# Loading the next group's x in halves behind stores, and another order of the last normalisations

## The chip, the cores and the metric

The kernel runs on one core of a Trainium2 chip. The metric is the device time of one execution in microseconds (us); six runs of the kernel before have a median of 277.8 us, from 277.44 to 279.92. The engines are named as the profile names them: PE (matrix multiply; PEld is its weight load), DVE (vector), ACT (scalar activations), POOL, and SP, whose queue issues nearly all transfers.

## What is computed

One cross-attention layer. x is (16, 256, 256), the context is (16, 77, 192), with 8 heads of 256 columns. All is float32.

```python
Q = (img_embed @ Wq).reshape(B, -1, H, D).transpose(0, 2, 1, 3)
K = (sent_embed @ Wk).reshape(B, -1, H, D).transpose(0, 2, 1, 3)
V = (sent_embed @ Wv).reshape(B, -1, H, D).transpose(0, 2, 1, 3)
score = jnp.einsum('bhqd,bhkd->bhqk', Q, K) / math.sqrt(D)
mask = (atten_mask != 0)[:, None, None, :]
score = jnp.where(mask, score, -jnp.inf)
attn = jax.nn.softmax(score, axis=-1)
ctx = jnp.einsum('bhqk,bhkd->bqhd', attn, V).reshape(B, -1, H * D)
out = ctx @ Wo + img_embed
mu = jnp.mean(out, axis=-1, keepdims=True)
var = jnp.var(out, axis=-1, keepdims=True)
return (out - mu) * jax.lax.rsqrt(var + EPS) * gamma + beta
```

## The kernel before

**Tiles and groups.** The 16 x 256 rows of x are 32 tiles of 128 rows, `t` = 0 to 31, two for each batch. Four batches (eight tiles) make a group `g` = 0 to 3. Each group of x is loaded twice: `load_x` (L140) brings the natural rows into `xg`, in one transfer of 1 MB; there the products are added and the result is normalised and stored. `load_xT` (L160) brings the same rows in an order from which a block transpose on DVE (`transpose_x`, L170) makes the transposed x for the scores; it is four transfers of 256 KB, 1 MB in all.

**Folded weights.** A start-up of some 54 us folds Wq with Wk (`gA`, `gB`) and Wv with Wo (`uA`, `uB`). After that each batch needs `a` (context times the first fold, `prepare_a`, a quarter of the next group's per step), `vw` (context times the second, `prepare_vw`), the scores, the softmax and the product with `vw`.

**The loop** (L857) has 16 steps, `b` = -1 to 14. Step `b` does the scores (L307) of the `new` tiles, those of batch b+1; DVE adds the mask's bias and takes the row maxima (`shift`, L323); ACT does the exponentials (L339); DVE sums and POOL scales (`weigh`, L346); DVE transposes the result (`turn`, L364). Meanwhile PE works at `vw` and `a` for later and then at the products of the `now` tiles, those of batch b: `seven` (L416) for batches 0 to 10, plain `attend` (L374) for the last five. The `old` tiles, those of batch b-1, get their statistics (`finish`, L479), their reciprocal deviation by two small ACT operations (`spread`, L492) and their normalisation (`normalise`, L522). Every engine works through its instructions in the order in which this code names them; that order is written by hand.

**Two ways to normalise.** The plain way is two DVE operations (L518 in `centre`, and L534). The way called `aside` takes the small factor `less` (L508, on POOL, or on DVE where `less_on` says so), one ACT operation (L528) and two POOL operations (L529, L530). When both tiles of a batch are done, a store of 256 KB is issued on SP (L541); the two last tiles are stored one by one (L946).

**The SP queue** works in order too: a store that waits for its normalisation holds up whatever is named behind it. A step counter `n = (b+1) % 4` places the preparation of the next group `g = (b+1)//4 + 1`. Both loads of that group are named in the step with n = 0 (L871), that is in steps -1, 3 and 7; the transposes of that x come in the steps with n = 2 (tiles 0 to 3 of the group) and n = 3 (tiles 4 to 7), late on DVE (L898). The scores of the group begin one step later. The natural rows are first read two steps after n = 3, by `add_product` (L475).

**The end.** In the last step (b = 14) `old` is tiles 26 and 27, `now` is 28 and 29, `new` is 30 and 31. The statistics of 26 and 27 stand between the exponentials of 30 and 31, and their normalisation behind `turn(30)` (L919). After the loop come the two last products and the last four normalisations: 28 and 31 on DVE, 29 and 30 aside.

Of the kernel before, what the change touches and what calls it, by code (L numbers as in the profile page):

```python
# [15 lines left out]
P = 128  # L16
# [37 lines left out]
def kernel(  # L54
# [13 lines left out]
    nc = tc.nc  # L68
    B, S, DI = x.shape
# [3 lines left out]
    NG = B // GB  # L73
    QT = S // P
    NT = B * QT
    GT = GB * QT
    NF = H // 2
    KR = S2 - KM
    BK = 32
    NM = P // BK  # L80
# [47 lines left out]
    xg_of = {}  # L128

    x_rows = x.rearrange("b (t p) d -> p (b t) d", p=P)  # L130
    out_rows = out.rearrange("b (t p) d -> p (b t) d", p=P)
    c_rows = c.rearrange("b k l -> (b k) l").rearrange("(r p) l -> p r l", p=CR)

    def flat(ap):
        return ap.rearrange("p a b -> p (a b)")
# [4 lines left out]
    def load_x(g):  # L140
        xg_of[g] = const.tile([P, GT, DI], F32, tag=f"xg{g}", name=f"xg_{g}")
        nc.sync.dma_start(xg_of[g], x_rows[:, g * GT : (g + 1) * GT, :])
# [12 lines left out]
    xT_of, a_of, vw_of, p_of, mv_of = {}, {}, {}, {}, {}  # L155

    def in_two(name, shape, g):
        return pools[g % 2].tile(shape, F32, tag=f"{name}{g % 2}", name=f"{name}_{g}", bufs=1)

    def load_xT(g):  # L160

        xT_of[g] = in_two("xT", [P, GT * NM, 2, BK], g)
        rows = x.rearrange("b s d -> (b s) d")[g * GT * P : (g + 1) * GT * P, :]
        rows = rows.rearrange("(m r) (i n) -> i r m n", r=BK, i=NM)
        for i in range(NM):
            nc.sync.dma_start(
                xT_of[g][i * BK : (i + 1) * BK].rearrange("p m n q -> p m (n q)"), rows[i]
            )

    def transpose_x(g, j):  # L170
# [136 lines left out]
    def scores(t):  # L307
        g = t // GT
        j, bl = t % GT, (t // QT) % GB
        ps = [ps_mm.tile([P, 512], F32, tag="mm", name=f"ps_{t}_{a}") for a in range(2)]  # L310
        for m in range(NM):
            for dc in range(2):
                for i in range(NM):
                    nc.tensor.matmul(  # L314
                        ps[m // 2][i * BK : (i + 1) * BK, m % 2 * 2 * S2 : (m % 2 + 1) * 2 * S2],
                        xT_of[g][:, j * NM + m, dc],
                        flat(a_of[g][:, dc, bl, 2 * i : 2 * i + 2, :]),
                        start=(dc == 0),
                        stop=(dc == 1),
                    )  # L320
        ps_of[t] = ps
# [153 lines left out]
    def add_product(t):  # L475
        y = xg_of[t // GT][:, t % GT, :]
        nc.vector.tensor_tensor(y, po_of.pop(t), y, ALU.add)  # L477

    def finish(t):  # L479
        if t in po_of:  # L480
            add_product(t)
        g, j = t // GT, t % GT
        y = xg_of[g][:, j, :]
        bn = st.tile([P, 6], F32, tag="bn", name=f"bn_{t}")
        nc.vector.bn_stats(bn, y)
        if j == 0:
            mv_of[g] = st.tile([P, GT, 2], F32, tag="mv", name=f"mv_{g}", bufs=2)
        nc.vector.bn_aggr(mv_of[g][:, j, :], bn)
# [3 lines left out]
    def spread(first, last):  # L492

        g, lo, hi = first // GT, first % GT, (last - 1) % GT + 1
        log = st.tile([P, GT], F32, tag="log", name=f"log_{first}")
        rstd = st.tile([P, GT], F32, tag="rstd", name=f"rstd_{first}")
        nc.scalar.activation(log[:, lo:hi], mv_of[g][:, lo:hi, 1], AF.Ln, bias=eps)
        nc.scalar.activation(rstd[:, lo:hi], log[:, lo:hi], AF.Exp, scale=-0.5)
        all_rstd_of[first, last] = rstd

    def invert(first, last, aside=(), less_on=nc.gpsimd):

        g = first // GT
        rstd = all_rstd_of.pop((first, last))
        if aside:
            less = st.tile([P, GT], F32, tag="less", name=f"less_{first}")
            for j in (t % GT for t in aside):
                less_on.tensor_scalar(  # L508
                    less[:, j : j + 1], mv_of[g][:, j, 0:1], rstd[:, j : j + 1], -1.0,
                    ALU.mult, ALU.mult,  # L510
                )
        for t in range(first, last):
            j = slice(t % GT, t % GT + 1)
            rstd_of[t] = rstd[:, j], less[:, j] if aside else None

    def centre(t):
        y = xg_of[t // GT][:, t % GT, :]
        nc.vector.scalar_tensor_tensor(  # L518
            y, y, mv_of[t // GT][:, t % GT, 0:1], gam, ALU.subtract, ALU.mult
        )  # L520

    def normalise(t, aside=False, centred=False):  # L522

        g, j = t // GT, t % GT
        rstd, less = rstd_of.pop(t)
        y = xg_of[g][:, j, :]
        if aside:
            nc.scalar.activation(y, y, AF.Identity, bias=less, scale=rstd)  # L528
            nc.gpsimd.tensor_tensor(y, y, gam, ALU.mult)  # L529
            nc.gpsimd.tensor_tensor(y, y, bet, ALU.add)  # L530
        else:
            if not centred:
                centre(t)
            nc.vector.scalar_tensor_tensor(y, y, rstd, bet, ALU.mult, ALU.add)  # L534
        if t >= NT - QT:
            return
        done.append(t)
        if t ^ 1 in done:
            t |= 1
            j |= 1  # L540
            nc.sync.dma_start(  # L541
                out_rows[:, t + 1 - QT : t + 1, :], xg_of[g][:, j + 1 - QT : j + 1, :]
            )
# [312 lines left out]
    last = NT - 1  # L856
    for b in range(-1, B - 1):  # L857
        old = range(max(b - 1, 0) * QT, b * QT)
        now = range(max(b, 0) * QT, (b + 1) * QT)
        new = range((b + 1) * QT, (b + 2) * QT)  # L860
        for t in new:
            scores(t)
        for t in new:
            shift(t)
        for n in range(0, 2) if b < 0 else range(b + 2, min(b + 3, B // 2)):
            turn_last(n)
        g, n = (b + 1) // GB + 1, (b + 1) % GB
        work = [prepare_vw(b + 1)]
        if g < NG:
            work.append(prepare_a(g, (n,)))  # L870
            if n == 0:  # L871
                load_xT(g)
                load_x(g)
        for part_A, _, _ in work:
            part_A()
        for _, part_B, _ in work:
            part_B()
        for i, t in enumerate(new):
            exponential(t)
            if old:  # L880
                finish(old[i])
            weigh(t)
        if old:
            spread(old[0], old[-1] + 1)
        for _, _, copies in work:
            for dst, src in copies():
                nc.scalar.copy(dst, src)  # L887
        if b + 1 < NS:
            differences(b + 1)
        if b < NS:  # L890
            if now:
                seven(b)
            if old:
                invert(old[0], old[-1] + 1)
                normalise(old[0])
            for t in new:
                turn(t)
            if n >= NF - 2:  # L898
                for j in range((n - NF + 2) * GT // 2, (n - NF + 3) * GT // 2, 2):
                    transpose_x(g, j)  # L900
            if old:
                normalise(old[1])
            if now:
                add_seven(b)
            if b + 1 < NS:
                sums(b + 1)
            continue
        for t in now:
            attend(t)
        if b < B - 2:  # L910
            invert(old[0], old[-1] + 1, aside=old[:1])
            normalise(old[0], aside=True)
            turn(new[0])
            normalise(old[1])
            turn(new[1])
            for t in now:
                add_product(t)
        else:
            turn(new[0])  # L919
            invert(old[0], old[-1] + 1, aside=old)  # L920
            for t in old:
                normalise(t, aside=True)
            turn(new[1])
            for t in now:
                finish(t)
            spread(now[0], now[-1] + 1)

    for t in new:  # L930
        attend(t)
    centre(last - 3)
    invert(last - 3, last - 1, aside=(last - 2,), less_on=nc.vector)
    normalise(last - 2, aside=True)
    finish(last - 1)
    spread(last - 1, last)
    normalise(last - 3, centred=True)
    invert(last - 1, last, aside=(last - 1,), less_on=nc.vector)
    normalise(last - 1, aside=True)
    finish(last)  # L940
    spread(last, NT)
    centre(last)
    invert(last, NT)
    normalise(last, centred=True)
    for t, queue in ((last - 1, nc.scalar), (last, nc.sync)):
        queue.dma_start(out_rows[:, t, :], xg_of[NG - 1][:, t % GT, :])  # L946


# [29 lines left out]
```

## Time and profile before

| what | value |
|---|---|
| median of six runs | 277.8 us |
| the profiled execution's own time | 279.26 us |
| its span in the trace | 277.4 us |
| lies around the span | 1.86 us |
| mean granted PE clock | 0.997 of full |
| bytes read / written | 17.57 MB / 4.19 MB |

Busy time of the engines in the span: PE 268.1 us (97%), DVE 210.5 (76%), POOL 160.9 (58%), ACT 131.4 (47%).

How to read it: a page of the profile shows one execution. A list of the chain of waits goes back from the last instruction, at each step to what released it; "issue" in it is time in which an engine waited for nothing that the profile shows. A view by windows gives, for chosen stretches, the busy time of each engine with the number of its instructions, the granted PE clock, the mean busy share of the 16 DMA engines (packets that overlap can take it above 1) and the rate in GB/s. A packet is counted whole in one window.

### The profile page before, as it was taken

To read this page: it belongs to the slowest core of one execution; us is meant where nothing else is said; L and a number is where in the kernel's file an instruction comes from. 1 tells how busy PE (TensorE), PEld (TensorE's weight loads), DVE (VectorE), ACT (ScalarE), POOL (GpSimd) and SP (SyncE) were. 2 spreads that over 40 slices of the span, in tenths; PEclk is the share of its full clock that TensorE was granted. 3 is DMA by queue.
4 is the path that set the end of the run, shared out by engine and by line. 5 is a ranking of instruction groups with operands and counts; after the bars stand their busy time and mean duration, and the time that the engine had idled before them with its cause. 6 is when DMAs were issued, how large, how long until landed. Compare 5 with 4: busy or idle time off the path is not lost.

```text
span 277.4 us, 13331 instructions
## 1 busy us (share of the span) xinstructions
PE 268.1 (97%) x5972; PEld 191.3 (69%) x5972; DVE 210.5 (76%) x406; ACT 131.4 (47%) x417; POOL 160.9 (58%) x221
## 2 busy tenths in 40 slices
PE   7999999999999999989999999899999999999992
PEld 7856487867595959486959595787777767584650
DVE  0363966697649898969798888678787978879885
ACT  2303212355728281817373736455554644827552
POOL 1000007919677878785878777677787537244284
PEclk9999999999999999999999999999999999999998
DMA  6987999992000102940101019400101010110103
GB/s 182 249 191 186 329 167 161 234 166 86 2 6 2 43 2 67 174 149 4 43 2 43 2 51 191 145 2 6 41 4 43 2 43 2 40 40 2 41 2 117
DMA packets 40202, 22.63 MB, mean 82 GB/s; under 512 B 23168, under 2 KB 38608, under 8 KB 40144
## 3 DMA queue, kind: packets, MB, share of 16 engines
q1 hardware_dynamic: 40000, 21.64, 36.1%
q8 instruction: 47, 0.77, 1.2%
q10 hardware_dynamic: 144, 0.13, 0.1%
q14 instruction: 11, 0.09, 0.1%
HBM read 17.57 MB, written 4.19 MB: 78 GB/s over the span
## 4 chain that ended last, share of the span: by engine, by line
PE 90%; DVE 3%; DMA 2%; ACT 2%; issue 1%; POOL 1%; SPq 0%; DVEq 0%; POOLq 0%
PE ps L314 24%; PE pa L197 12%; PE pv L239 9%; PE po L430 9%; PE pm L430 7%; PE pa L211 6%; PE pv L250 6%; PE po L379 5%; PE pu L704 3%; PE pr L273 2%; DMA wq_nat<-in_L_xattn_Wq_dram 2%; ACT e L343 2%; PE pg L747 1%; PE pgb L704 1%; PE pw L718 1%
## 5 line engine op out<-in xcount | busy, mean ns | idle before, releaser
L343 ACT ACTIVATE e<-s,top 128x77 f32<-128x77 f32 x256 | 67.2, 347 | 74.1 <-DVE top L336 74.1
L357 POOL TENSOR_TENSOR p<-e,rden 128x512 f32<-128x512 f32 x64 | 47.3, 759 | 48.7 <-DVE rden L351 39.9
L314 PE MATMUL ps<-a,xT 128*32 128x154 f32 x2048 | 70.5, 294 | 0.8 <-issue 0.8
L314 PEld LDWEIGHTS ps<-a,xT 128*32 128x32 f32 x2048 | 66.2, 110 | 2.9 <-issue 2.0
L329 DVE TENSOR_TENSOR s<-ps,bias 128x308 f32<-128x308 f32 x64 | 30.3, 476 | 19.4 <-PE ps L314 19.4
L197 PE MATMUL pa<-cA,gA 128*32 128x308 f32 x512 | 36.1, 423 | 0.0
L463 POOL TENSOR_TENSOR xg<-xg,m 128x256 f32<-128x256 f32 x33 | 24.2, 732 | 12.6 <-DVE xg L477 10.9
L197 PEld LDWEIGHTS pa<-cA,gA 128*32 128x32 f32 x512 | 17.7, 110 | 19.6 <-issue 7.1
L239 PE MATMUL pv<-uA,cA 128*32 128x512 f32 x256 | 30.7, 592 | 0.0
L367 DVE STREAM_TRANSPOSE pT<-p 128x640 f32<-128x640 f32 x32 | 25.5, 817 | 2.4 <-POOL p L357 2.3
L349 DVE TENSOR_REDUCE den<-e 128x8 f32<-128x616 f32 x32 | 24.7, 772 | 3.4 <-ACT e L343 3.4
L336 DVE TENSOR_REDUCE top<-s 128x8 f32<-128x616 f32 x32 | 25.4, 795 | 1.1
L887 ACT COPY vw<-pv 128x512 f32<-128x512 f32 x32 | 17.1, 586 | 8.7 <-PE pv L250 8.7
L534 DVE SCALAR_TENSOR_TENSOR xg<-xg,rstd,bet 128x256 f32<-128x256 f32 x25 | 19.5, 782 | 2.2 <-ACT vw L887 0.5
L393 POOL TENSOR_TENSOR ts<-vw 128x768 f32<-128x768 f32 x11 | 20.2, 1839 | 0.0
L211 PE MATMUL pa<-cB,gB 64*32 64x308 f32 x512 | 19.5, 420 | 0.0
L379 PE MATMUL po<-vw,pT 128*32 128x256 f32 x320 | 19.2, 380 | 0.0
L477 DVE TENSOR_TENSOR xg<-po,xg 128x256 f32<-128x256 f32 x32 | 12.1, 413 | 7.6 <-PE po L430 7.2
L211 PEld LDWEIGHTS pa<-cB,gB 64*32 64x32 f32 x512 | 9.7, 107 | 11.3 <-issue 7.6
L250 PE MATMUL pv<-uB,cB 64*32 64x512 f32 x256 | 17.4, 601 | 0.0
L430 PE MATMUL po<-vr,pT 128*32 128x128 f32 x352 | 16.2, 273 | 1.2 <-issue 1.2
L887 ACT COPY a<-pa 128x308 f32<-128x308 f32 x48 | 16.8, 455 | 0.0
(112 smaller groups left out, 382.3 us busy)
## 6 DMA issues: line engine op xcount, KB each, us to landing
xT<-in_x_dram SPq DMA_DIRECT2D x16, 256.0 KB, 8.1
xg<-in_x_dram SPq DMA_DIRECT2D x4, 1024.0 KB, 9.5
out_dram<-xg SPq DMA_DIRECT2D x15, 256.0 KB, 2.3
wo<-in_L_xattn_Wo_dram SPq DMA_DIRECT2D x4, 512.0 KB, 5.2
wvT<-in_L_xattn_Wv_dram SPq DMA_DIRECT2D x16, 96.0 KB, 3.2
wq_nat<-in_L_xattn_Wq_dram SPq DMA_DIRECT2D x2, 512.0 KB, 6.3
wq_blk<-in_L_xattn_Wq_dram SPq DMA_DIRECT2D x8, 128.0 KB, 4.7
wk_blk<-in_L_xattn_Wk_dram SPq DMA_DIRECT2D x8, 96.0 KB, 5.8
```

The lines of the kernel that those rows point to most:

```text
L197: nc.tensor.matmul(flat(o[i * BK : (i + 1) * BK]), gA[:, h, cols(dc, i)], flat(cA[:, batches, :]), start=not B_first, stop=B_first,)
L211: nc.tensor.matmul(flat(banks[j + k][i * BK : (i + 1) * BK]), gB[half(k), h % NF, cols(dc, i)], flat(cB[half(k), batches, :]), start=B_fir ...
L239: nc.tensor.matmul(pv[k][i * BK : (i + 1) * BK], cA[:, b, k * BK : (k + 1) * BK], uA[:, parts, :, i], start=True, stop=False,)
L250: nc.tensor.matmul(pv[k][i * BK : (i + 1) * BK], cB[half(k), b, k * BK : (k + 1) * BK], uB[half(k), parts, :, i], start=False, stop=True,)
L314: nc.tensor.matmul(ps[m // 2][i * BK : (i + 1) * BK, m % 2 * 2 * S2 : (m % 2 + 1) * 2 * S2], xT_of[g][:, j * NM + m, dc], flat(a_of[g][:, ...
L329: nc.vector.tensor_tensor(s[:, a * H // 2 : (a + 1) * H // 2], ps[a][:, : H // 2 * S2].rearrange("p (h k) -> p h k", k=S2), bias[:, b, :]. ...
L343: nc.scalar.activation(e[:, h], s[:, h], AF.Exp, bias=top[:, h : h + 1])
L357: nc.gpsimd.tensor_tensor(part, e_mh[:, :, :, keys], rden_mh.unsqueeze(3).to_broadcast(list(part.shape)), ALU.mult,)
L367: nc.vector.transpose(pT_of[t].rearrange("p n m q -> p m n q"), p.rearrange("p m (n k) -> p m n k", k=BK),)
L379: nc.tensor.matmul(po[i * BK : (i + 1) * BK], pT[:, n, i], vw_of[b][:, 2 - n // 2 * 2 : 4 - n // 2 * 2, n % 2, :] if n < NF else vr[:, b, ...
L430: nc.tensor.matmul(out[i * BK : (i + 1) * BK], weight[:, i], moving, start=(n == 0), stop=(n == len(terms) - 1),)
L887: nc.scalar.copy(dst, src)
```

## The change

`load_xT` takes a range of tiles. The loads leave the step with n = 0. The first half of the transposed x is loaded in the step with n = 1, the second with n = 2, and the natural rows with n = 3; each is named behind `normalise(old[1])`, so behind that step's store in SP's order. In the last step, tiles 26 and 27 get statistics and the aside normalisation before the `shift` of 30 and 31. Tile 28's statistics come between the two last `turn`s. After the loop 28 and 29 are normalised aside, 30 and 31 by DVE, and both last stores go to SP.

```diff
-    def load_xT(g):
+    def load_xT(g, lo=0, hi=GT):
-        xT_of[g] = in_two("xT", [P, GT * NM, 2, BK], g)
-        rows = x.rearrange("b s d -> (b s) d")[g * GT * P : (g + 1) * GT * P, :]
+        if lo == 0:
+            xT_of[g] = in_two("xT", [P, GT * NM, 2, BK], g)
+        rows = x.rearrange("b s d -> (b s) d")[(g * GT + lo) * P : (g * GT + hi) * P, :]
         rows = rows.rearrange("(m r) (i n) -> i r m n", r=BK, i=NM)
         for i in range(NM):
             nc.sync.dma_start(
-                xT_of[g][i * BK : (i + 1) * BK].rearrange("p m n q -> p m (n q)"), rows[i]
+                xT_of[g][i * BK : (i + 1) * BK, lo * NM : hi * NM].rearrange(
+                    "p m n q -> p m (n q)"
+                ),
+                rows[i],
             )
...
         for t in new:
             scores(t)
+        if b == B - 2:
+            for t in old:
+                finish(t)
+            spread(old[0], old[-1] + 1)
+            invert(old[0], old[-1] + 1, aside=old)
+            for t in old:
+                normalise(t, aside=True)
         for t in new:
             shift(t)
...
             work.append(prepare_a(g, (n,)))
-            if n == 0:
-                load_xT(g)
-                load_x(g)
...
             exponential(t)
-            if old:
+            if old and b < B - 2:
                 finish(old[i])
             weigh(t)
-        if old:
+        if old and b < B - 2:
             spread(old[0], old[-1] + 1)
...
             if old:
                 normalise(old[1])
+            if n == NF - 1:
+                load_x(g)
+            elif n:
+                load_xT(g, (n - 1) * GT // 2, n * GT // 2)
             if now:
                 add_seven(b)
...
             turn(new[0])
-            invert(old[0], old[-1] + 1, aside=old)
-            for t in old:
-                normalise(t, aside=True)
+            finish(now[0])
+            spread(now[0], now[1])
             turn(new[1])
-            for t in now:
-                finish(t)
-            spread(now[0], now[-1] + 1)
     for t in new:
         attend(t)
-    centre(last - 3)
-    invert(last - 3, last - 1, aside=(last - 2,), less_on=nc.vector)
-    normalise(last - 2, aside=True)
-    finish(last - 1)
-    spread(last - 1, last)
-    normalise(last - 3, centred=True)
-    invert(last - 1, last, aside=(last - 1,), less_on=nc.vector)
-    normalise(last - 1, aside=True)
-    finish(last)
-    spread(last, NT)
-    centre(last)
-    invert(last, NT)
-    normalise(last, centred=True)
-    for t, queue in ((last - 1, nc.scalar), (last, nc.sync)):
-        queue.dma_start(out_rows[:, t, :], xg_of[NG - 1][:, t % GT, :])
+    add_product(last - 2)
+    for t in (last - 3, last - 2):
+        invert(t, t + 1, aside=(t,), less_on=nc.vector)
+        normalise(t, aside=True)
+        if t < last - 2:
+            finish(t + 1)
+            spread(t + 1, t + 2)
+    for t in (last - 1, last):
+        finish(t)
+        spread(t, t + 1)
+        centre(t)
+        invert(t, t + 1)
+        normalise(t, centred=True)
+        nc.sync.dma_start(out_rows[:, t, :], xg_of[NG - 1][:, t % GT, :])
```

## The prediction, made before the changed kernel was run

> **What bounds the kernel now.** I read the page first, then the chain of waits in order of time, then windows around its odd pieces, then the timeline of the end. The page says PE, with one DMA queue to remember:
>
> ```profile
> PE 268.1 (97%) x5972; PEld 191.3 (69%) x5972; DVE 210.5 (76%) x406; ACT 131.4 (47%) x417; POOL 160.9 (58%) x221
> ...
> DMA  6987999992000102940101019400101010110103
> ...
> q8 instruction: 47, 0.77, 1.2%
> ```
>
> PE runs 2 x 5972 = 11,944 matmuls and weight loads. Queue 8 moves 0.77 MB in 47 packets: 16 KB each, 64 bytes for each PE instruction. So the queue can be read as PE's program, arriving in pages of about 256 instructions. The DMA row has two late stretches of load, slices 17-18 and 25-26; these are the loads of groups 2 and 3.
>
> From 54 us on, the chain is PE alone, step after step, but for two pieces:
>
> ```profile
> 120.72 1.16 PE ps L314 x33
> 121.87 0.84 issue
> 122.71 3.21 PE ps L314 x92
> ...
> 176.09 1.30 PE po L430 x46
> 177.39 1.17 issue
> 178.56 1.17 PE po L430 x33
> ```
>
> Twice PE stands still, in the middle of a group of matmuls with no data to wait for. The windows of whole steps show the price, and single tenths of a microsecond show what arrived before PE went on:
>
> ```profile
> 106.62:120.72 14.10, 14.10 (x376) 10.35 (x372) 11.92 (x24) 7.65 (x25) 10.95 (x14) 1.00 0.94 171
> 120.72:135.97 15.25, 14.41 (x376) 11.28 (x372) 11.85 (x23) 7.64 (x25) 10.91 (x14) 1.00 0.07 22
> 135.97:150.07 14.10, 14.10 (x376) 10.35 (x372) 12.43 (x25) 7.65 (x25) 11.06 (x14) 1.00 0.07 22
> 164.17:179.73 15.56, 14.39 (x376) 10.37 (x372) 11.51 (x22) 7.54 (x25) 10.82 (x14) 1.00 0.86 171
> ...
> 119.90:120.00 0.10, 0.10 (x14) 0.10 (x7) 0.10 (x1) 0.00 (x0) 0.06 (x1) 1.00 1.56 399
> 142.60:142.70 0.10, 0.10 (x8) 0.00 (x0) 0.10 (x2) 0.10 (x2) 0.00 (x0) 1.00 0.76 164
> 176.00:176.10 0.10, 0.10 (x12) 0.10 (x8) 0.10 (x2) 0.00 (x0) 0.10 (x1) 1.00 0.80 195
> ```
>
> The first column is the length of the stretch, then busy time and count of PE, PEld, DVE, ACT, POOL, then clock, DMA share, GB/s. 164 GB/s in 0.1 us is one page of 16 KB, seen alone at 142.6. The same extra shows at 119.9 and at 176.0, and PE resumes 2.76 and 2.51 us after them. Both follow a load of 2 MB that fills the DMA engines from about 108 to 120.2 and from 165 to about 175.4. So I take both stops to be PE out of program, its page having stood in the DMA engines behind x.
>
> A step without trouble takes 14.10 us; the two bad ones 15.25 and 15.56, and the one after the second 14.21 (193.94 - 179.73). Lost: 1.15 + 1.46 + 0.11 = **2.72 us**.
>
> **The loads.** 2 MB in one burst become 0.5, 0.5 and 1 MB, a step apart. The burst at 107 shows the rates: the transposed x at some 155 GB/s (112 to 117 us), the natural x at 289 GB/s (117 to 120.3). A half is then 0.5 / 0.155 = 3.4 us plus a ramp of about 1.5, the natural rows 3.5 us, each behind a store of about 1 us, against 12 us before. SP issues 28 transposed-x transfers for 16, 0.38 to 3.78 us each; behind them on SP stand only stores, the next one a step later. Hidden.
>
> Nothing is late for data. A half is issued just after its step's store, some 0.5 us into the next PE step, and its transposes on DVE stand at +12 us in that step (147.99 against a step start of 135.97); landing at +7 leaves 5 us. The natural rows of group 1 are issued near 107 and read near 133. Group 1's first half has no store before it (step 0 has no old tiles), so SP issues it near 49 us, as now.
>
> What is left is whether a small burst traps a page. Pages seen in quiet steps sit at +0.2, +3.7, +11.2 us in the step from 92.52 and drift later by about 0.5 us a step (142.6 and 148.2 are +6.7 and +12.2 in the step from 135.97), until they wrap. From 118.3 (expected) to 119.9 and from 172.3 to 176.0 they were late by 1.6 and 3.7 us, about what was left of x in the engines. [...] I take **0.2**; the ends for this term are 0 and 1.15, the smaller of the stops seen.
>
> [...]
>
> **The end.** It starts from this, in the timeline:
>
> ```profile
> 259.77 4.20 ACT L343 ACTIVATE e<-s,top 128x77 f32<-128x77 f32 x16 [3.27 <-DVE top L336]
> ...
> 271.88 0.20 DVE L508 TENSOR_SCALAR less<-mv,rstd 128x1 f32<-128x1 f32 x1
> 272.03 0.42 DVE L477 TENSOR_TENSOR xg<-po,xg 128x256 f32<-128x256 f32 x1
> ...
> 273.60 0.79 POOL L530 TENSOR_TENSOR xg<-xg,bet 128x256 f32<-128x256 f32 x1
> 273.91 0.76 DVE L534 SCALAR_TENSOR_TENSOR xg<-xg,rstd,bet 128x256 f32<-128x256 f32 x1
> ...
> 274.69 0.35 SPq L946 DMA_DIRECT2D out_dram<-xg  x1
> ```
>
> PE's last matmul ends at 271.96, so until then what moves is free if it feeds PE in time. Tiles 26 and 27 now put four DVE operations (0.42 + 0.18 + 0.42 + 0.18 = 1.2 us) before `shift(30)`; it had idle time, and its row maxima come about 0.4 late. On ACT two small operations (0.49) and two of 0.6 stand before the exponentials; counted from DVE's 258.4 through POOL's `less` they end near 260.4, so the exponentials start 0.7 late. Then `turn(30)` ends near 266.4, where PE takes it at 267.46, and `turn(31)`, behind tile 28's statistics, near 268.2 against 269.62. Cover 1.0 and 1.4 us; without it each further delay is paid in full. POOL's four operations on 26 and 27 (3.1 us) end near 263.2, before the scaling of 30 at 263.7.
>
> On DVE, `finish(30)` still starts near 270.15 (tile 29's `less` waits for ACT as before). Then comes `centre(30)` (0.71) and its second operation (0.72) where there was tile 28's second operation and a `less`: done at 272.6 instead of 272.08, so tile 31 starts **0.5 late**. Afterwards POOL is idle, where it now works beside DVE: L518 then takes 0.43 (its minimum) for 0.64, L534 0.49 for 0.76. That returns **0.4**: the first is partly hidden by ACT's two operations (ends 273.69), so 0.15 + 0.27. Only one store stays open at the end. Net **+0.1**, between -0.2 (the store gains) and +0.7 (nothing returned, the maximum of both waits).
>
> **Sum.** 279.26 - 2.72 + 0.2 + 0.1 = 276.8 on the profiled execution's scale. That execution took 1.46 us more than the median, and the six runs spread over 2.5 us. If the 1.46 is a heavier dose of the stops, a median run has only 2.72 - 1.46 = 1.26 to lose and goes to the same 276.8. If it is the cost of being profiled, a median run loses all and goes to 277.8 - 2.42 = 275.4. Nothing shown decides; I take the middle, **276.1 us**.
>
> **Rivals.** (1) *The stops are not there in ordinary runs, or are not pages* (the profiler's own traffic, or something that no view shows): 277.8 + 0.1 = 277.9. For it: one execution is all I see, and its time is above the median. Against: the page before each restart. (2) *The stops multiply, slower*: eight steady bursts instead of two. If each small burst holds a page past its spare time, five at 1.15 us give 277.8 + 5.75 - 2.72 + 0.1 = 280.9; from four stops on it is slower than before by over 0.5%. [...] Against: the first 8 us of both old bursts began at the same place and stopped nothing. (3) *The gain stands, but only the heavier half is there to win*: 276.8 and a little above, the forecast's upper end. That the loads aren't really parted can happen only for group 1's first half.
>
> **How the numbers follow.** Forecast 0.67, rival 1 0.15, rival 2 (with an end that goes badly) 0.18. What a measurement of this kernel can tell from no change is about 0.5%: 276.4 to 279.2. Of the forecast, 0.55 lies below 276.4 and 0.12 (rival 3) above; so faster 0.55, same 0.12 + 0.15 = 0.27, slower 0.18. The likeliest's own range is 275.2 to 277.0; for 8 in 10 it is widened to 275.0 and to 278.2, which takes in rival 1 and the bad end of the tail and leaves out rival 2.
>
> **What would show it.** Right: the chain has no "issue" piece of PE after 54 us, all steps from 78 to 222 us take 14.10, the DMA row has eight small peaks instead of two blocks, and DVE's last L534 takes 0.5 us and ends some 2.7 us earlier. The exponentials of 30 start 0.7 later against PE, with no gap on PE behind them. Wrong: pieces of "issue" inside steps that begin with a burst, or a clean trace with an unchanged median; a gap on PE before tile 30's or 31's product would unmake the part on the end.

## The result: 0.57% faster, and PE no longer stops

The changed kernel takes 276.69 us (median of 22 runs, 276.13 to 278.38); the kernel before, run beside it, 278.41 us (46 runs, 277.37 to 280.0). The ratio is 0.9943, interval 0.9930 to 0.9956. The profiled execution of the changed kernel has a span of 276.6 us and a time of its own of 278.38 us, the longest of the 22; why is told below.

First the profile's page: busy engines, the DMA share in 40 slices, and the queue that the prediction reads as PE's program.

```profile
PE 267.8 (97%) x5972; PEld 189.3 (68%) x5972; DVE 210.3 (76%) x406; ACT 131.7 (48%) x419; POOL 160.4 (58%) x221
...
DMA  5985999930000131410130506000405060110112
...
q8 instruction: 47, 0.77, 1.2%
```

The two late blocks of load are now small separate peaks. That queue still has 47 packets, 0.77 MB. The chain of waits, in order of time, shows the two places where PE stood still before; line numbers have moved by 5:

```profile
122.69 4.19 PE ps L319 x128
...
176.91 2.18 PE po L435 x80
179.09 4.19 PE ps L319 x128
```

The scores are one piece of 128 matmuls, po one of 80, and no piece called "issue" stands between PE's pieces from 50 us to 269 us. The windows of the same steps (length first, then busy time and count of PE, PEld, DVE, ACT, POOL, clock, DMA share, GB/s):

```profile
122.69:136.79 14.10, 14.10 (x376) 10.35 (x372) 11.86 (x23) 7.64 (x25) 10.97 (x14) 1.00 0.08 23
164.99:179.09 14.10, 14.10 (x376) 10.35 (x372) 11.51 (x22) 7.54 (x25) 10.84 (x14) 1.00 0.32 96
```

Both take 14.10 us, where they took 15.25 and 15.56. The timeline of the end (start, duration, engine, operation):

```profile
271.54 0.41 DVE L482 TENSOR_TENSOR xg<-po,xg 128x256 f32<-128x256 f32 x1
271.83 2.29 SPq L956 DMA_DIRECT2D out_dram<-xg  x2
...
272.67 0.48 DVE L523 SCALAR_TENSOR_TENSOR xg<-xg,mv,gam 128x256 f32<-128x256 f32 x1
...
273.26 0.48 DVE L539 SCALAR_TENSOR_TENSOR xg<-xg,rstd,bet 128x256 f32<-128x256 f32 x1
```

PE's last matmul ends at 271.21 here. Tile 31 starts 0.33 us after it (0.07 before), and its last two DVE operations take 0.48 each (0.64 and 0.76 before). From the start of tile 30's scores to the end of the last operation: 18.22 us, 18.40 before.

**Adding up single executions.** In every profile of this study the execution's own time comes apart into four parts: the start of the first scores, the time lost to PE's stops (each step's length above 14.10, or 11.38 late in the loop), the end as just measured, and a rest, which lies between 204.01 and 204.31 us.

| kernel | own time | first scores | lost | end | rest |
|---|---|---|---|---|---|
| before | 279.26 | 54.01 | 2.72 | 18.40 | 204.13 |
| changed | 278.38 | 55.98 | 0 | 18.22 | 204.18 |
| parted loads alone | 278.20 | 55.49 | 0 | 18.40 | 204.31 |
| new end alone | 277.57 | 53.86 | 1.48 | 18.22 | 204.01 |
| x moved | 278.88 | 54.58 | 1.77 | 18.39 | 204.14 |
| x twice | 281.05 | 55.39 | 3.04 | 18.39 | 204.23 |
| x midstep | 278.46 | 53.81 | 2.13 | 18.21 | 204.31 |
| transposed x whole | 277.49 | 54.96 | 0 | 18.40 | 204.13 |
| fewer instructions | 278.00 | 54.97 | 0.60 | 18.39 | 204.04 |
| 30 aside | 277.33 | 54.78 | 0 | 18.25 | 204.30 |

So the changed kernel's profiled execution is long because its first scores began at 55.98 us, 1.97 us later than in the profile before. That start varies from 53.8 to 56.0 us, in start-up code that is the same in nine of the ten kernels (run 7 leaves twelve transposes out). It is not ordered by where the loads of x stand; what makes it vary was not studied.

### The profile page after: what moved, and what is told of

The parts are those of the page before. It is cut to its first block, busy times and chain, and to the rows that moved or that the text cites. A ratio compares the mean times of both kernels' runs of the same rounds, so it can differ in the third digit from the quotient of the medians.

```text
span 276.6 us, 13362 instructions
## 1 busy us (share of the span) xinstructions
PE 267.8 (97%) x5972; PEld 189.3 (68%) x5972; DVE 210.3 (76%) x406; ACT 131.7 (48%) x419; POOL 160.4 (58%) x221
## 4 chain that ended last, share of the span: by engine, by line
PE 93%; DMA 3%; DVE 2%; SPq 1%; issue 0%; DVEq 0%
PE ps L319 24%; PE pa L202 12%; PE pv L244 10%; PE po L435 9%; PE pm L435 7%; PE po L384 7%; PE pa L216 6%; PE pv L255 6%; DMA wk_last<-in_L_xattn_Wk_dram 3%; PE pu L709 3%; PE pr L278 2%; PE pgb L709 1%; PE pw L723 1%; PE pr L290 1%; PE phb L723 1%; PE ph L766 1%
## 5 line engine op out<-in xcount | busy, mean ns | idle before, releaser
L202 PEld LDWEIGHTS pa<-cA,gA 128*32 128x32 f32 x512 | 16.4, 110 | 20.9 <-issue 8.0
L384 PEld LDWEIGHTS po<-vw,pT 128*32 128x32 f32 x320 | 10.0, 110 | 9.5 <-DVE den L354 2.5
```

What stands on the lines that cost most here:

```text
L202: nc.tensor.matmul(flat(o[i * BK : (i + 1) * BK]), gA[:, h, cols(dc, i)], flat(cA[:, batches, :]), start=not B_first, stop=B_first,)
L384: nc.tensor.matmul(po[i * BK : (i + 1) * BK], pT[:, n, i], vw_of[b][:, 2 - n // 2 * 2 : 4 - n // 2 * 2, n % 2, :] if n < NF else vr[:, b, ...
```

## Experiments

A *heap*, below, is what stands of x in the DMA engines at one time. The *spare time* of a page is what it may be late without a stop of PE; with the lateness that the prediction read, the two stops of the kernel before leave 1.6 - 0.84 = 0.8 us and 3.7 - 1.17 = 2.5 us for it, an estimate. Several experiments changed only one of the two parts of the change; others changed the size or the place of a heap.

**1. The parted loads alone.** The end is the old one; `load_xT` takes a range of tiles, as in the change.

```diff
-            if n == 0:
-                load_xT(g)
-                load_x(g)
...
                 normalise(old[1])
+            if n == NF - 1:
+                load_x(g)
+            elif n:
+                load_xT(g, (n - 1) * GT // 2, n * GT // 2)
```

> The kernel before with the parted loads alone; the order of the end is the old one. Theory (PE's stops are pages of its program held behind 2 MB of x): nearly the whole gain is here, ratio to the kernel before 0.9945 (0.9925 to 0.9960), no piece of "issue" on PE in the steps after the start-up, the last DVE operation ends 18.4 us after the scores of tile 30 begin, as before. Rival (the gain comes from the end, the stops being a thing of single executions): ratio 0.999 to 1.000.

Measured: 277.22 us against 278.36, ratio 0.9964 (0.9943 to 0.9984). No stop in the trace, end 18.40 us. The mechanism is as expected; the ratio lies just outside the expected range (to 0.9960), its interval reaches well into it. The rival falls: this part alone removes the stops.

**2. The new end alone.**

```diff
+        if b == B - 2:
+            for t in old:
+                finish(t)
+            spread(old[0], old[-1] + 1)
+            invert(old[0], old[-1] + 1, aside=old)
+            for t in old:
+                normalise(t, aside=True)
...
+            finish(now[0])
+            spread(now[0], now[1])
             turn(new[1])
```

(with the changed kernel's other edits to the last step and its code behind the loop, and the loads as before)

> The kernel before with the new order of the end alone; the loads are the old ones. Theory: ratio 0.9995 (0.998 to 1.001), from the end's 0.18 us; PE still stops in the steps of the two late loads, 0.5 to 1.6 us each. Rival (the end makes the gain): ratio 0.994 to 0.996.

Measured: 277.62 us against 278.36, ratio 0.9977 (0.9955 to 1.0). The end takes 18.22 us in the trace; the interval holds the 0.9995 expected and does not settle the size. The stops are there, smaller in this execution: the first is only 0.23 us of step length and no piece of the chain; the second lengthens two steps by 1.25 us in all. That speaks against the rival, whose 0.996 the ratio's interval alone, from 0.9955, does not quite exclude. The chain of waits shows the second stop:

```profile
175.02 1.30 PE po L430 x46
176.32 0.54 issue
```

It is at the same 46th matmul of po as in the kernel before.

**3. The natural rows moved, the transposed x left in place.**

```diff
             if n == 0:
                 load_xT(g)
-                load_x(g)
...
                 normalise(old[1])
+            if n == NF - 1:
+                load_x(g)
```

> The kernel before with one move: the natural rows are loaded at the end of the step with n = 3, behind its store; the transposed x stays whole (1 MB) in the step with n = 0. Theory (a page is late by what is left in the DMA engines, and only the 2 MB heap reaches the pages with 1 us to spare): 1 MB of transposed x is through by some +9.5 us of its step, before those pages, so no stop or one below 0.5 us; ratio 0.994 to 0.9965. Rival (the transposed x has to be halved too): both stops remain in part, ratio 0.997 to 1.000.

Measured: 278.12 us against 278.36, ratio 0.9980 (0.9955 to 1.0004). The expectation was wrong, and the queue of SP and the chain say why:

```profile
164.06 0.42 SPq L142 DMA_DIRECT2D xg<-in_x_dram  x1
164.57 7.92 SPq L166 DMA_DIRECT2D xT<-in_x_dram  x4
```

```profile
176.17 1.30 PE po L430 x46
177.48 0.69 issue
```

The end of a step with n = 3 is the start of one with n = 0. Group 2's natural rows were issued just ahead of group 3's transposed x, and the heap was 2 MB again, in the other order. PE stopped at the same 46th matmul. The heap one group earlier, issued from 107.92 us, left no stop: its steps took 14.10 us. So this run did not part the heap; run 6 does. The ratio lies in the rival's range, but the rival's reason, that the transposed x has to be halved, falls with run 6.

**4. One load made larger.**

```diff
         nc.sync.dma_start(xg_of[g], x_rows[:, g * GT : (g + 1) * GT, :])
+        if g == 2:
+            again = const.tile([P, GT, DI], F32, tag="xg3", name="again")
+            nc.sync.dma_start(again, x_rows[:, g * GT : (g + 1) * GT, :])
```

> The kernel before with the natural rows of group 2 read twice in its burst (3 MB for 2), the second time into a buffer that is loaded over later and never read. Theory: the engines drain some 3.5 us later, the page that was late by 1.6 us is late by about 5, the step after the load takes 17.5 to 19 us for 15.25, ratio 1.008 to 1.014. Rival (a stop is a fixed price of a load, 0.8 to 1.2 us): step 15 to 15.6 us, ratio 0.999 to 1.002.

Measured: 281.05 us against 278.36, ratio 1.0089 (1.0058 to 1.0121). The ratio is in the expected range; the step is not. Chain and windows around the stop:

```profile
122.09 1.16 PE ps L317 x33
123.25 1.50 issue
```

```profile
122.09:138.01 15.92, 14.42 (x377) 11.31 (x372) 11.85 (x23) 7.64 (x25) 10.91 (x14) 1.00 0.13 40
122.30:122.40 0.10, 0.10 (x12) 0.10 (x5) 0.10 (x1) 0.00 (x0) 0.00 (x0) 1.00 1.67 481
```

PE stops at the same 33rd matmul, for 1.50 us instead of 0.84; the step takes 15.92, not 17.5 to 19. The page (the extra in the second row) shows at 122.3, 14.3 us into the step from 107.99 and 1.1 us before the heap's full rate ends at 123.4. In the changed kernel's same step it shows 11.5 us in (120.1 against a start of 108.59): it is 2.8 us late, of 3.9 us that the heap still took from when it was due. More load makes the stop longer, but the page does not wait for the whole heap. That the ratio came out in its range is luck: this execution lost 3.04 us to stops, 1.5 more than a median run before (1.54, estimated below), and the measured difference is 2.7 us. In this execution most of the remainder is a late start of the first scores, 55.39 us (54.29 in that estimate).

**5. The same 1 MB at another place in the step.** To get there, the load is issued on ACT's queue instead of SP's.

```diff
-        nc.sync.dma_start(xg_of[g], x_rows[:, g * GT : (g + 1) * GT, :])
+        queue = nc.scalar if g else nc.sync
+        queue.dma_start(xg_of[g], x_rows[:, g * GT : (g + 1) * GT, :])
...
+        if g < NG and n == NF - 1:
+            load_x(g)
         for _, _, copies in work:
             for dst, src in copies():
                 nc.scalar.copy(dst, src)
...
-            if n == NF - 1:
-                load_x(g)
-            elif n:
+            if 0 < n < NF - 1:
                 load_xT(g, (n - 1) * GT // 2, n * GT // 2)
```

> The changed kernel with one edit: the natural rows of groups 1 to 3 are issued from ACT behind the exponentials of the step with n = 3, some 8 us into the step, where the changed kernel issues them from SP at its end. The size of each heap stays, its place moves to where seven meets the scores and a page has 1 us to spare. Theory (place decides along with size): PE stops once or twice for 0.3 to 1 us each near the end of those steps, at a page boundary; ratio to the kernel before 0.9955 to 0.999. Rival (heaps of 1 MB are harmless wherever they fall): no stop, ratio 0.993 to 0.9955.

Measured: 278.75 us against 278.39, ratio 1.0016 (1.0000 to 1.0031). The chain of waits shows two stops; the windows show the step behind group 2's load, and the page that came late before the first stop:

```profile
106.42 0.63 PE ps L320 x17
107.05 1.00 issue
...
220.54 0.37 PE ps L320 x9
220.91 0.50 issue
```

```profile
164.13:178.24 14.11, 14.11 (x377) 10.36 (x372) 11.51 (x22) 7.54 (x25) 10.82 (x14) 1.00 0.07 22
...
105.40:105.50 0.10, 0.10 (x16) 0.10 (x8) 0.10 (x1) 0.00 (x0) 0.08 (x1) 1.00 0.73 174
```

Two stops, 1.00 and 0.50 us idle, 1.31 and 0.81 us of step; group 2's load, of the same size, costs 0.01 us. The page at 105.4 is 13.1 us into its step, where the changed kernel has it at 11.0: 2.1 us late, shown when the heap has just gone through. In the step of the second stop it is due 11.1 us in and shows 12.6 us in. In that of group 2's load it is due only 12.7 us in, when such a heap is nearly through. That load went through ACT's queue as well, so the queue alone does not make the stops. The rival falls: 1 MB cost nothing at the start of a step in run 1 (steps of 14.10) and 1.31 us here, ahead of the stretch with the most PE instructions in a microsecond: from 119.65 us on, po and the scores are 208 matmuls in 6.37 us, 33 in a microsecond, where the 96 from 126.02 us on take 5.85 us, 16 in a microsecond. The price was under-estimated; this move alone gives back the whole gain.

**6. Two parts instead of three.**

```diff
-            if n == 0:
-                load_xT(g)
-                load_x(g)
...
                 normalise(old[1])
+            if n == 1:
+                load_xT(g)
+            elif n == NF - 1:
+                load_x(g)
```

> The kernel before with its loads parted in two, not in three: the transposed x whole (1 MB) behind the store of the step with n = 1, the natural rows behind that of the step with n = 3; nothing else changed. Theory: the transposed x is through by some +9 us of its step, its pages have 2 to 4 us to spare, so no stop, and the time is that of the run with the parted loads alone: ratio 0.9945 to 0.9975. Rival (halving is needed): a stop in the step of the transposed x, ratio 0.9975 to 1.000.

Measured: 276.96 us against 278.39, ratio 0.9947 (0.9922 to 0.9972). No stop in the trace, all its steps 14.10, end 18.40 as in the old order. Halving the transposed x is not what pays; keeping it apart from the natural rows is. The 2 to 4 us to spare were the author's estimate; this run, without a stop, does not show them.

**7. The program shifted by 24 instructions.** Twelve of the first warm-up transposes, whose result is not used, are left out.

```diff
-        keep_busy(14)
+        keep_busy(2)
```

> The kernel before without 12 of its 14 warm-up transposes at the start (they compute nothing that is used), so 24 PE instructions fewer ahead of everything. Theory (a stop is a page boundary): the stops move 12 matmuls later in the program, from behind the 33rd to behind the 45th matmul of the scores in the step after group 2's load, and from behind the 46th to behind the 58th matmul of po in the step of group 3's load, if this execution stops there at all. Rival (a stop is set by time or by what PE works at): they stay at the 33rd and the 46th, or fall anywhere.

Measured in one execution: 278.00 us. This execution has no stop in the step after group 2's load, and a short one in that of group 3's. The timeline of the weight loads, of which there is one to each matmul:

```profile
176.04 0.24 PEld L430 LDWEIGHTS po<-vr,pT 128*32 128x32 f32 x8
176.26 0.46 PEld L430 LDWEIGHTS po<-vw,ss 128*32 128x32 f32 x16
176.69 0.24 PEld L430 LDWEIGHTS po<-vr,pT 128*32 128x32 f32 x8
176.91 0.44 PEld L430 LDWEIGHTS po<-ts,pT 128*32 128x32 f32 x10
177.60 0.12 PEld L430 LDWEIGHTS po<-ts,pT 128*32 128x32 f32 x3 [0.25 <-issue]
```

With the 16 of the first product, the gap stands behind number 16 + 8 + 16 + 8 + 10 = 58. It was 46 in four kernels; it moved by 12, as the program did. Counted from the start of the program, 3794 matmuls stand ahead of the gap in all five.

**8. The changed kernel with tile 30 aside again.**

```diff
-    for t in (last - 1, last):
-        finish(t)
-        spread(t, t + 1)
-        centre(t)
-        invert(t, t + 1)
-        normalise(t, centred=True)
-        nc.sync.dma_start(out_rows[:, t, :], xg_of[NG - 1][:, t % GT, :])
+    finish(last - 1)
+    spread(last - 1, last)
+    invert(last - 1, last, aside=(last - 1,), less_on=nc.vector)
+    normalise(last - 1, aside=True)
+    finish(last)
...
+    normalise(last, centred=True)
+    for t, queue in ((last - 1, nc.scalar), (last, nc.sync)):
+        queue.dma_start(out_rows[:, t, :], xg_of[NG - 1][:, t % GT, :])
```

> The changed kernel with tile 30 normalised aside again (ACT and POOL) and its store on ACT's queue; tile 31 stays on DVE. Theory (the end's gain is DVE working beside an idle POOL, 0.44 us, less the 0.26 us that tile 31 starts late): from the start of tile 30's scores to the last DVE operation 18.35 to 18.45 us, as in the kernel before. Rival (26 and 27 ahead of the exponentials make the gain): 18.15 to 18.25 us, as in the changed kernel.

Measured in one execution: 277.33 us, end 18.25 us. The theory falls, the rival holds: tile 30's engine is worth 0.03 us. The timeline shows where the gain is:

```profile
270.55 0.72 POOL L534 TENSOR_TENSOR xg<-xg,gam 128x256 f32<-128x256 f32 x1 [0.49 <-ACT xg L533]
...
271.22 0.48 DVE L523 SCALAR_TENSOR_TENSOR xg<-xg,mv,gam 128x256 f32<-128x256 f32 x1
271.35 0.93 POOL L535 TENSOR_TENSOR xg<-xg,bet 128x256 f32<-128x256 f32 x1
...
271.81 0.76 DVE L539 SCALAR_TENSOR_TENSOR xg<-xg,rstd,bet 128x256 f32<-128x256 f32 x1
```

POOL's first operation on tile 30 begins 0.54 us after PE's last matmul (270.01) where in the kernel before it began 0.84 after (272.80 against 271.96). It is out of DVE's way when `centre(31)` comes, which takes 0.48 for 0.64. So the earlier work on 26 to 29 gives 0.15 us, and tile 30 on DVE gives the late start of tile 31 back almost as it takes it.

## Why the prediction was right

**The mechanism held.** The stops read as page boundaries of PE's program. Shown by run 7, in one execution, where the program moved by 12 matmuls and the stop with it, and by the distances between stops: from the 33rd matmul of one step's scores to the 46th of po three steps later are 2810 matmuls and weight loads, 10.98 pages of 256; from run 5's first stop to the 33rd matmul, one step on, 768, or 3.00 pages; between run 5's two stops 5872, or 22.94. To whole numbers 6, 0 and 16 instructions are missing. The trace of the kernel before has 6 more PE instructions between its two stops, semaphores at L197 (4) and L314 (2), which makes 2816, or 11.00 pages; in run 5 they were not counted. That traffic sets a stop's size is shown by run 4 (1.50 us behind 3 MB, 0.84 behind 2), that place does by run 5 (1.00 and 0.50 us, and none behind group 2's load), and that the parting of the loads removes the stops by runs 1 and 6 (no stop, steps of 14.10).

A count in the trace of the kernel before says the same: 17 packets of the program's queue stand ahead of the late one of 119.9, and 28 ahead of that of 176.0, while PE had done 4778 and 7588 matmuls and weight loads at the stops, 18.7 and 29.6 pages. From one to the other 11 packets came for 2810 of them, 255 to a packet. At each stop PE had done 1.7 and 1.6 pages more than the packets ahead of the late one hold. A page that showed 2.1 us late in run 5 stopped PE for 1.00 us.

**The stops in an ordinary run.** The prediction could not tell whether the 1.46 us by which the profiled execution stood above the median was a heavier dose of stops or the cost of being profiled, and took the middle. With 46 runs the median is 278.41, so it stood 0.85 us above. With a rest of 204.18, the median before leaves 278.41 - 204.18 - 18.40 = 55.83 us for start and stops, the median after 276.69 - 204.18 - 18.22 = 54.29. If starts are alike, a median run lost 1.54 us to stops, where the profiled execution lost 2.72: a heavier dose, the first reading. This is an estimate. A cost of being profiled stays open, since the table holds profiled executions only; in the eight kernels with several runs the profiled one is above its median by 0.6 us on average.

**The number, and the luck in it.** The forecast of 276.1 is 0.6 us below the 276.69 measured. All of that is the reference, 277.8 us by six runs and 278.41 by 46. The gain forecast, 1.7 us, is the gain measured, 1.72, but three errors cancel in it: 1.99 us for the stops (the middle) where a median run lost some 1.54, 0.2 for the small bursts where 0 came, and +0.1 for the end where it was -0.18. The end of the last DVE operation came 0.93 us earlier in the profiled executions, not 2.7, because of the late start (2.72 + 0.18 - 1.97).

**Small bursts hold pages too, at no cost.** 0.2 us were taken, with ends 0 and 1.15. No run shows this term: the changed kernel lost 0, with steps of 14.10 us, and a page was held all the same. Behind group 2's natural rows it shows 5.3 us into the step from 164.99:

```profile
170.30:170.40 0.10, 0.10 (x8) 0.10 (x4) 0.10 (x1) 0.10 (x2) 0.10 (x1) 1.00 0.91 256
```

In run 5, which has no load of x there, it shows 2.5 us in (166.6 against 164.13). Held by 2.8 us, it stopped nothing. The late page of each step, which PE needs where `seven` meets the scores, comes when the small bursts are through, and stands where the quiet steps had put it (11.0, 11.5, 12.0, 12.3 and 12.7 us into successive steps). Run 5 gives the spare time there: pages 2.1 and 1.5 us late, stops of 1.00 and 0.50 us, which leaves 1.1 and 1.0 us, an estimate.

**"About what was left of x in the engines."** This step was too simple. In run 4 the page went through 1.1 us ahead of the end of the heap; in run 5 it came at its end. The page of 176.0 was also less late than the 3.7 us of the working: run 5's step from 164.13, without the heap, has it 9.1 us in, which makes it 2.8 us late. These errors cost nothing here, since the small bursts had time to spare either way.

**The end.** +0.1 us was taken, between -0.2 and +0.7; it measured -0.18. Tile 31 started 0.26 us later relative to PE, not 0.5, because `finish(30)` came 0.28 us earlier than the 270.15 of the working; the 0.44 us that DVE gets back beside an idle POOL was right (0.4). The exponentials of 30 came 0.40 us later against the scores than before (predicted 0.7), and PE had no gap behind them, as predicted.

**Data in time, the rivals.** In the changed kernel's trace no engine waits for a load after 60 us; the only wait for a transfer is SP's for the last store (1.4 us). Rival 1 falls with runs 1, 5 and 6, whose medians move as the traces say, and with run 7. Rival 2, the stops that multiply, is what run 5 makes happen with another place for the same bytes; the changed kernel avoids it. (Its sum took the profiled execution's 2.72 us off the median of 277.8; by the first reading 1.26 would have to go off, which gives 282.4.) Rival 3 is in part what the estimate above supports: a median run had less to lose than the profiled execution, and 276.69 is next to its 276.8. But what was there was won: no trace of runs 1, 6 and 8 or of the changed kernel has a stop left.

## What to carry to other kernels

In this kernel what reads as PE's program, 47 packets of 16 KB, came late behind bulk loads: 1.6 us behind 2 MB in the kernel before, as the prediction read it, and 2.8 us behind 3 MB in run 4. Where an engine at 97% stands still with no releaser, compare the place of the stop with bulk loads some microseconds earlier, and count instructions between stops: whole multiples of a page, 256 PE instructions here, point to the program. Then part large loads and place each so that it ends before the stretch in which that engine has the most instructions in a microsecond; how large a load may be was here a question of that place (three loads of 1 MB cost 1.31, 0.01 and 0.81 us of step in run 5, and nothing in run 1).

## What had not been expected of the hardware

- From the middle of the 0.1 us in which a late page shows to PE's restart passed 2.76 and 2.51 us in the kernel before, 2.51 in run 2, 2.82 in run 3, 2.40 in run 4 and 2.60 in run 5: much the same under heaps of 1, 2 and 3 MB. Counted from the end of the page's packet in the trace it is 1.41 and 1.37 us in the kernel before, and 1.31 to 1.53 us in the eight stops of 0.5 us or more of these kernels.
- The start of the first scores varied by 2.2 us between executions of the same start-up code, more than the whole gain of the change. Single profiled times of these kernels can therefore not be compared; lengths of steps, equal to 0.01 us, can. What makes the start vary was not studied.
- A stop cost about 0.3 us more step length than the idle piece in the chain shows (1.15 for 0.84, 1.31 for 1.00, 0.81 for 0.50).
